# One store per layer moved from SyncE's queue to GpSimd's

## The chip, the cores and the metric

The kernel runs on 1 core of one Trainium2 chip. Its engines are TensorE (PE in the profile; PEld is its loading of weights), VectorE (DVE), ScalarE (ACT), GpSimd (POOL) and SyncE (SP). Each has its own list of instructions; SP only starts transfers. SP, ACT and POOL each start DMAs from their own queue, and 16 DMA engines carry them out. The metric is device microseconds of an execution.

## The reference

The input x has 8 batches of 512 tokens with 256 values. There are two layers, and each is a mixer followed by a mixture of experts; each adds its result to x:

```python
x = x + _L0_attn_a_ref(_layernorm(x, axis=-1), ...)   # a scan with decay 0.9 over the tokens
x = x + _L0_ffn_ref(_layernorm(x, axis=-1), ...)      # 16 experts, 4 chosen, and a shared one
x = x + _L0_attn_b_ref(_layernorm(x, axis=-1), ...)   # causal attention, 16 heads
x = x + _L0_ffn_ref(_layernorm(x, axis=-1), ...)
```

The mixture of experts is what matters here. The router chooses 4 of 16 experts for every token; a shared pair of experts works on all of them:

```python
h = jnp.einsum('td,edf->etf', x, gate_w)
u = jnp.einsum('td,edf->etf', x, up_w)
y = jnp.einsum('etf,efd->etd', jax.nn.silu(h) * u, down_w)
routed = jnp.einsum('etd,te->td', y, combine)
sh = jax.nn.silu(x @ sh_gate_w) * (x @ sh_up_w) @ sh_down_w
return (routed + sh).reshape(hidden_states.shape)
```

## The kernel before, in words

The kernel works in four stages: a *stretch* and a *routed* stage for each layer.

A stretch (`stretch`) goes through the 8 batches. For each it does the mixer (scan in the first layer, attention in the second), norms the result, computes the router's choices, and scatters each token's row into a table in device memory, `xg`, sorted by expert (POOL, indirect DMAs at L662). The sum after the mixer is stored to the first of two tables in device memory, `parts[i][0]` (SP, L1209). The shared experts (`shared_experts`) run two batches later: products with the gate and up weights (L908), their activation (L921 to L927), the product with the down weights into the accumulator tile `pd_m` (L936), two ACT copies of it into the tile `ys_m` (L944), and the store of `ys_m`, 512 KB, into the second table, `parts[i][1]` (L945). So 8 such stores belong to each layer. The last one stands at the end of the stretch: after it the list of blocks is ready (`blocks`), and nothing else of the stretch is left.

A routed stage (`routed`) reads a count of blocks on every engine (L886), skips a branch for a rare surplus of blocks (L889), and goes through 136 blocks of 128 sorted rows. For each block SP reads where its rows lie (L779, a register load for four blocks at a time) and loads them into a tile `rows` (L793); ACT and DVE copy the expert's weights into `gate` and `up` (L801); PE transposes the rows (L808), ACT copies the result (L809), PE multiplies with gate and up (L819), ACT and DVE form the activation (L827 to L829), PE multiplies with the down weights (L847), ACT scales (L855), and POOL adds the rows into `parts[i][0]` or `parts[i][1]`, by turns, with an indirect accumulating DMA (L856). At the start the first two blocks' rows are loaded at once, and both blocks are transposed on PE ahead of the first product.

The order on each engine is made when the program is built, from the order in the source and a planner's estimates; waits between engines are semaphores that are put in by what each instruction reads and writes. Tiles come from pools with a fixed number of buffers: `ys_m`, the shared experts' activations `act_m` and the `rows` tiles share one pool of 9 buffers (`kb4`), so that a new tile waits until the last use of its buffer's former holder is over. Each DMA signals its completion on one of 8 semaphores by turns, with one set of 8 for SP's and ACT's queues and another for POOL's.

Of the kernel before, what the change touches and what calls it, by code (L numbers as in the profile page):

```python
# [16 lines left out]
B, T, D = 8, 512, 256  # L17
# [57 lines left out]
def tile_hybrid_block(  # L75
# [22 lines left out]
    nc = tc.nc  # L98
# [8 lines left out]
    def bank(shape, name: str, kind: str = "one"):  # L107
        kind = instead.get(kind, kind)
        return stage[kind].tile(shape, FP, tag=kind, name=name)
# [15 lines left out]
    parts = [[dram.tile([NTOK + BLK, D], FP, name=f"part_{i}_{j}") for j in range(2)] for i in range(2)]  # L125
# [11 lines left out]
    def rows_of(part, b: int):  # L137
        return part[b * T : (b + 1) * T, :].rearrange("(t p) d -> p t d", p=P)
# [51 lines left out]
    def load_expert(e: int):  # L190
# [13 lines left out]
        out=before,  # L204
        in_=before,
# [17 lines left out]
    def load_attention_weights():  # L223
# [16 lines left out]
        out=causal, in_=causal, compare_op=ALU.is_ge, fill=0.0, base=0, pattern=[[0, 2], [1, P]], channel_multiplier=-1  # L240
# [6 lines left out]
        out=tri, in_=tri, compare_op=ALU.is_gt, fill=0.0, base=0, pattern=[[1, P]], channel_multiplier=-1  # L247
# [162 lines left out]
    def kb4(name: str):  # L410
        return work.tile([P, NT, D], FP, tag="kb4", name=name, bufs=KB)
# [481 lines left out]
    def shared_experts(i: int, b: int, xnT_of, tanh: bool):  # L893

        tag = f"m{i}_{b}"

        def steps():
            xnT = xnT_of()
            acts = []
            for n in range(NSH):  # L900
                _, g_sb, u_sb, _ = shared[n]
                act = work.tile([P, KF, T], FP, tag="kb4", name=f"act_{tag}_{n}", bufs=KB)
                acts.append(act)
                for f in range(KF):
                    pair = [bank([P, T], f"pg_{tag}_{n}_{f}_{which}") for which in range(2)]
                    for dst, w in zip(pair, (g_sb, u_sb)):
                        for k in range(KD):
                            nc.tensor.matmul(  # L908
                                dst,
                                lhsT=w[:, k, f * P : (f + 1) * P],  # L910
                                rhs=xnT[:, k, :],
                                start=(k == 0),
                                stop=(k == KD - 1),
                            )
                        if dst is pair[0]:
                            yield KD * T
                    ph, pu = pair
                    sig = work.tile([P, T], FP, tag="col", name=f"sig_{tag}_{n}_{f}", bufs=COLS)
                    if tanh:

                        nc.scalar.activation(sig, ph, AF.Tanh, scale=0.5)  # L921
                        nc.vector.scalar_tensor_tensor(sig, sig, 1.0, ph, ALU.add, ALU.mult)
                        nc.vector.scalar_tensor_tensor(act[:, f, :], sig, 0.5, pu, ALU.mult, ALU.mult)
                    else:
                        nc.scalar.activation(sig, ph, AF.Sigmoid)
                        nc.vector.tensor_mul(sig, ph, sig)
                        nc.vector.tensor_mul(act[:, f, :], pu, sig)  # L927
                    yield KD * T
            y_sb = kb4(f"ys_{tag}")
            for half in range(2):  # L930
                py = bank([P, 2, D], f"pd_{tag}_{half}")
                for j in range(2):
                    t = 2 * half + j
                    for n in range(NSH):
                        for f in range(KF):
                            nc.tensor.matmul(  # L936
                                py[:, j, :],
                                lhsT=acts[n][:, f, t * P : (t + 1) * P],
                                rhs=shared[n][3][:, f, :],
                                start=(n == 0 and f == 0),  # L940
                                stop=(n == NSH - 1 and f == KF - 1),
                            )
                    yield NSH * KF * D
                nc.scalar.copy(y_sb[:, 2 * half : 2 * half + 2, :], py)  # L944
            nc.sync.dma_start(out=rows_of(parts[i][1], b), in_=y_sb)  # L945

        return Piece(NSH * KF * (2 * KD * T + NT * D), steps())


# [485 lines left out]
```

## Time and profile before

| | us |
|---|---|
| median of 3 runs (lowest, highest) | 1792.99 (1790.45, 1796.93) |
| the profiled execution, its own time | 1789.56 |
| its span, first to last instruction | 1787.8 |
| PE busy | 1686.6 |
| DVE busy | 1094.7 |
| ACT busy | 806.1 |
| POOL busy | 769.6 |
| the last store of the first layer's shared sums starts | 375.06 |
| the last store of the second layer's | 1356.90 |

The mean granted clock of PE over the span is 0.975 of full speed. Times in the profile are microseconds from the span's start. A row of the timeline has the start, the length, the engine, the source line, the operation, what it writes and reads, how often, and in brackets how long the engine was idle before it and what ended that. Lines marked SPq, ACTq or POOLq are of an engine's sequencer (starting a DMA, waiting, loading a register), which are not counted as busy. A DMA's landing is the time from the start of its issue to the last of its completion signals. The profile names at each wait the signal that came last.

### The profile page before, as it was taken

The page shows a single profiled execution, that of the slowest core. Times are in us where ns is not written, and L with a number is a line of the kernel's source. Part 1 is how long each engine was busy: PE and PEld are TensorE (multiplying, and loading weights), DVE is VectorE, ACT ScalarE, POOL GpSimd, SP SyncE. Part 2 cuts the span into 40 slices and gives each one's busy share as a digit, 9 for nine tenths or more (in the row PEclk, how much of TensorE's full clock was granted, in tenths as well). Part 3 has the DMA queues.
Part 4 walks back from the last instruction along what each step waited for, and adds up shares of the span by engine and source line. Part 5 has one row for each costly group of instructions (what it writes and reads, how often), then busy time and mean ns, then how long its engine had stood idle before and what let it go on. Part 6 is the DMA issues. An engine that isn't in the chain of part 4 may idle for free. (4 is left out here: it accounts for less than half of the span.)

```text
span 1787.8 us, 32810 instructions
## 1 busy us (share of the span) xinstructions
PE 1686.6 (94%) x10640; PEld 1261.9 (71%) x10640; DVE 1094.7 (61%) x3399; ACT 806.1 (45%) x1740; POOL 769.6 (43%) x675
## 2 busy tenths in 40 slices
PE   5899999989999999979999999999998999999993
PEld 3566566569999999954445455455467999998993
DVE  5877777535555655546776675756653665565552
ACT  2322222135555555545654554544413555555552
POOL 4255554625555655540022422312442555555563
PEclk9899999999999999989999999999999999999997
DMA  5443322535555655540012112112443555566666
GB/s 167 154 148 133 130 78 84 198 76 94 97 95 102 111 98 95 96 89 10 28 50 73 63 61 73 51 60 80 149 172 78 93 98 94 110 125 122 127 122 177
DMA packets 149999, 181.37 MB, mean 101 GB/s; under 512 B 16097, under 2 KB 136961, under 8 KB 149825
## 3 DMA queue, kind: packets, MB, share of 16 engines
q0 software_dynamic: 54432, 81.53, 24.2%
q1 hardware_dynamic: 93600, 93.50, 17.6%
q10 hardware_dynamic: 1792, 4.19, 0.6%
q8 instruction: 89, 1.46, 0.3%
q14 instruction: 86, 0.70, 0.1%
HBM read 81.62 MB, written 97.53 MB: 100 GB/s over the span
## 5 line engine op out<-in xcount | busy, mean ns | idle before, releaser
L856 POOL DMA_INDIRECT part<-rows x272 | 427.0, 1570 | 370.0 <-ACT rows L855 291.4
L662 POOL DMA_INDIRECT xg<-sorted_m,slots_m x256 | 255.7, 999 | 283.4 <-ACT slots_m L659 116.6
L819 PEld LDWEIGHTS ph<-rows,gate 128*128 128x128 f32 x2176 | 286.3, 193 | 16.5 <-ACT rows L809 2.1
L819 PE MATMUL ph<-rows,gate 128*128 128x128 f32 x2176 | 290.0, 277 | 0.6 <-ACT rows L809 0.6
L819 PE MATMUL ph<-rows,up 128*128 128x128 f32 x2176 | 288.7, 276 | 0.0
L847 PE MATMUL pyr<-w_all,rows 128*128 x1088 | 280.5, 380 | 0.4 <-DVE rstd_l L398 0.4
L819 PEld LDWEIGHTS ph<-rows,up 128*128 128x128 f32 x2176 | 266.3, 193 | 0.0
L827 ACT ACTIVATE rows<-ph 128x256 f32<-128x256 f32 x272 | 104.2, 383 | 329.6 <-PE ph L819 329.6
L828 DVE TENSOR_TENSOR rows<-ph,rows 128x256 f32<-128x256 f32 x272 | 115.2, 423 | 190.3 <-ACT rows L827 190.0
L847 PEld LDWEIGHTS pyr<-w_all,rows 128*128 128x128 f32 x1088 | 185.2, 191 | 14.6 <-ACT rows L855 0.7
L801 ACT COPY gate<-w_all 128x512 f32 x272 | 170.0, 626 | 14.6 <-SPq L889 2.6
L1053 ACT ACTIVATE w_all<-ps_a 128x1024 f32<-128x1024 f32 x128 | 124.4, 1021 | 80.3 <-PE ps_a L1042 72.7
L801 DVE COPY up<-w_all 128x512 f32 x272 | 120.1, 442 | 33.0 <-PE ph L819 18.0
L855 ACT ACTIVATE rows<-pyr,gain 128x256 f32<-128x256 f32 x272 | 128.4, 472 | 14.7 <-PE pyr L847 13.2
L908 PE MATMUL pg_m<-xT_m,su_sb 128*128 128x512 f32 x256 | 131.4, 637 | 0.0
L832 DVE SCALAR_TENSOR_TENSOR gain<-rows,expert_b 128x4 f32<-128x4 f32 x272 | 61.2, 225 | 112.3 <-ACT rows L855 83.4
L1042 PE MATMUL ps_a<-w_all 32*128 32x512 f32 (+3 forms) x1024 | 122.1, 472 | 7.0 <-ACT w_all L1053 5.6
L908 PE MATMUL pg_m<-xT_m,sg_sb 128*128 128x512 f32 x256 | 123.0, 603 | 0.0
L936 PE MATMUL pd_m<-sd_sb,act_m 128*128 128x256 f32 x512 | 120.9, 385 | 0.0
L808 PE MATMUL pt<-ident,rows 128*128 128x128 f32 x544 | 105.1, 275 | 16.4 <-DMA rows<-xg 16.4
L829 DVE TENSOR_TENSOR rows<-ph,rows 128x256 f32<-128x256 f32 x272 | 115.1, 423 | 8.3
L936 PEld LDWEIGHTS pd_m<-sd_sb,act_m 128*128 128x128 f32 x512 | 97.1, 192 | 21.6 <-issue 4.7
(219 smaller groups left out, 2216.2 us busy)
## 6 DMA issues: line engine op xcount, KB each, us to landing
rows<-xg SPq DMA_DIRECT2D x272, 136.0 KB, 2.6
part<-x SPq DMA_DIRECT2D x16, 512.0 KB, 2.8
part<-ys_m SPq DMA_DIRECT2D x16, 512.0 KB, 2.8
w_all<-in_L_ffn_gate_w_dram SPq DMA_DIRECT2D x24, 256.0 KB, 5.2
w_all<-in_L_ffn_up_w_dram SPq DMA_DIRECT2D x24, 256.0 KB, 5.5
w_all<-in_L_ffn_down_w_dram SPq DMA_DIRECT2D x24, 256.0 KB, 5.9
sum<-part POOLq DMA_DIRECT2D x10, 512.0 KB, 4.2
xg<-zeros SPq DMA_DIRECT2D x34, 136.0 KB, 2.2
```

The lines of the kernel that those rows point to most:

```text
L662: nc.gpsimd.indirect_dma_start(out=xg[i], out_offset=bass.IndirectOffsetOnAxis(ap=slots[:, at : at + 1], axis=0), in_=rows[:, t, :], in_of ...
L801: copy(here, w_all[:, bass.ds(held[n][0] + half * KD * F, KD * F)])
L819: nc.tensor.matmul(ph[:, s, f * P : (f + 1) * P], lhsT=both[s][:, k * F + f * P : k * F + (f + 1) * P], rhs=rows[:, ROW + k * P : ROW + (k ...
L828: nc.vector.tensor_mul(act, ph[:, 0, :], act)
L829: nc.vector.tensor_mul(act, ph[:, 1, :], act)
L847: nc.tensor.matmul(py, lhsT=act[:, f * P : (f + 1) * P], rhs=w_all[:, bass.ds(w + 2 * KD * F + f * D, D)], start=(f == 0), stop=(f == KF - 1),
L855: nc.scalar.mul(rows[:, 0:D], py, gain[:, TK : TK + 1])
L856: nc.gpsimd.indirect_dma_start(out=parts[i][n % 2], out_offset=bass.IndirectOffsetOnAxis(ap=rows[:, D + 2 * TK : D + 2 * TK + 1].bitcast(U ...
L908: nc.tensor.matmul(dst, lhsT=w[:, k, f * P : (f + 1) * P], rhs=xnT[:, k, :], start=(k == 0), stop=(k == KD - 1),)
L936: nc.tensor.matmul(py[:, j, :], lhsT=acts[n][:, f, t * P : (t + 1) * P], rhs=shared[n][3][:, f, :], start=(n == 0 and f == 0), stop=(n == ...
L1042: nc.tensor.matmul(ps[j // 2][:, j % 2, col : col + n], lhsT=k_sb[w][r, o, c * P : (c + 1) * P], rhs=q_sb[r, o, c * P : T], start=True, st ...
L1053: nc.scalar.activation(es[two], ps[two][:, :, 0:cols], AF.Exp, scale=ATT_SCALE)
```

## The change

In each layer the last batch's `ys_m` is stored by POOL's queue; the other seven remain on SP's. What is stored and where stays the same.

```diff
                 nc.scalar.copy(y_sb[:, 2 * half : 2 * half + 2, :], py)
-            nc.sync.dma_start(out=rows_of(parts[i][1], b), in_=y_sb)
+
+            (nc.gpsimd if b == B - 1 else nc.sync).dma_start(out=rows_of(parts[i][1], b), in_=y_sb)
 
         return Piece(NSH * KF * (2 * KD * T + NT * D), steps())
```

In the built program the store is taken out of SP's list, where it stood ahead of the load of the block count (L886), and put into POOL's, between the last scatter (L662) and the load of the block count there. ACT's list is the same. In PE's list one register load (L772) moves past one block's down products in each layer, and in DVE's list a few small neighbours near the start of each routed stage change places. The completion semaphores that later DMAs use move on by one on POOL's queue and back by one on SP's.

## The prediction

> **What bounds the kernel now.** I read the page first: its span, the busy shares, the chain that ended last. Then, because the change touches one store per layer, the timeline of SyncE (SP) and TensorE (PE) around the end of each stretch, and last the durations and landings of DMAs of 512 KB by queue.
>
> ```profile
> span 1787.8 us, 32810 instructions
> PE 1686.6 (94%) x10640; PEld 1261.9 (71%) x10640; DVE 1094.7 (61%) x3399; ACT 806.1 (45%) x1740; POOL 769.6 (43%) x675
> PE 21%; DMA 2%; ACT 0%; issue 0%; SPq 0%; DVE 0%; ACTq 0%; POOL 0%; POOLq 0%; DVEq 0%
> ```
>
> PE is busy 94% of the span, so an edit on queues is worth what it does to PE's idle stretches. Of those over 5 us there are three in the trace; two are the ones right behind the moved store. The chain is named for the last 430 us alone; followed back it ends at the second of these two. This is its start, in order of time (start, length, what):
>
> ```profile
> 1358.47 1.13 SPq L779
> ...
> 1360.02 0.35 SPq L793
> ...
> 1360.94 2.05 DMA rows<-xg
> 1362.99 0.14 issue
> 1363.13 0.66 PE pt L808 x2
> ```
>
> The reader is to see that the chain runs over SP: a register load (L779), the loads of the first two blocks of sorted rows (L793), the second one's landing, and then PE's second pair of transposes (L808). The second block's landing decides, not the first's: in PE's order both blocks are transposed ahead of the first product (L819). The same stretch, timeline of SP, then of PE, then of PE after the first layer:
>
> ```profile
> 1356.90 0.38 SPq L945 DMA_DIRECT2D part<-ys_m  x1
> 1360.02 4.10 SPq L793 DMA_DIRECT2D rows<-xg  x5
> ```
> ```profile
> 1362.31 0.66 PE L808 MATMUL pt<-ident,rows 128*128 128x128 f32 x2 [6.06 <-DMA rows<-xg]
> 1363.13 0.66 PE L808 MATMUL pt<-ident,rows 128*128 128x128 f32 x2 [0.16 <-DMA rows<-xg]
> ```
> ```profile
> 380.39 0.66 PE L808 MATMUL pt<-ident,rows 128*128 128x128 f32 x2 [5.98 <-DMA rows<-xg]
> 381.31 0.66 PE L808 MATMUL pt<-ident,rows 128*128 128x128 f32 x2 [0.26 <-DMA rows<-xg]
> ```
>
> In layer 1 the store goes out at 375.06, the two loads at 378.15 and 379.08, the second lands at 381.17. From there on PE is the bound (100.00 us busy of the 100 from 400 to 500, 120.00 of the 120 from 1380 to 1500), so a shift of this start reaches the end one for one, once in each layer.
>
> **The change part by part.**
>
> *Removed from SP: one wait and one issue per layer.* SP's store waits for ScalarE's last copy (L944, ends 1356.87) and takes 0.38 us. Behind it stand the load of the block count (L886, 0.28), a branch with its semaphore waits (L889, 0.7 us in all) and the 1.13 us load of the row numbers: 3.12 us from the store's start to the first rows. Their data has been ready since about 1344. Without the store SP runs through all this while PE still multiplies, and stands at the first rows load, which by the built program waits for PE's last product (its buffer held an operand). PE ends at about 1356.25, so the first rows load goes at about 1356.4 in place of 1360.02: 3.6 us earlier.
>
> *The second rows load gains none of it by right.* It takes the buffer of the stored sum itself: in the built program it waits for the store's completion. Before, that store was long enough ago: it landed 3.41 us after 1356.90, at 1360.31, and SP came at 1360.94. After, SP will stand there waiting, so the start is: store's start + its landing + about 0.2 (in the routed stage a row load followed the landing that freed its buffer, 396.46, at 396.66) + 2.1 (landing of the load, 2.05 to 2.16). This replaces a wait of SP on SP by one on GpSimd's (POOL's) queue. Queued behind it on SP are the third and later rows loads, due on PE only after two blocks of products, at 1368.6: slack of over 3 us.
>
> *Added to POOL: one wait and one issue per layer.* The store stands behind the last scatter (L662, over at 364.7 and 1346.5) and ahead of the block count and branch; the first accumulate (L856) comes at 392.41 and 1373.19, so 16 us cover the store's issue on POOL, and would have to be used up before it costs. Behind the store stands also POOL's step that credits its skipped semaphores (1.0 and 1.6 us), for which the third rows load waits; about 1 us of load and branch and this step end near 1360, before that load is due.
>
> *The unknown: how long a 512 KB store takes from POOL's queue to land.* No row shows this store there. Rows, by source line (landing as min/median/max):
>
> ```profile
> L1327 POOL DMA_DIRECT2D out_dram<-sum x5: 1167/1173/1328, 1577.2 to 1761.4; - x5
> DMA to landing us min/median/max: 4.0/4.6/4.6
> ```
> ```profile
> L1317 POOL DMA_DIRECT2D sum<-part x10: 585/588/1182, 1555.6 to 1748.0; - x10
> DMA to landing us min/median/max: 3.8/4.2/5.3
> ```
> ```profile
> part<-ys_m SPq DMA_DIRECT2D x16, 512.0 KB, 2.8
> x<-part POOLq DMA_DIRECT2D x2, 512.0 KB, 4.4
> ```
>
> Lower end 2.75 (the quickest landing of the same store from SP; a queue that issues in 0.36 us is no slower than one that takes 0.6 to 1.3, unless the trace hides it). Upper end 5.3 (the longest 512 KB on POOL's queue). I take 4.4: the two kinds nearest are the writes L1327 (4.0 to 4.6, other row length) and the loads L1150 (4.3 to 4.6, same 128x4x256 shape, other direction).
>
> Layer 1: 375.1 + 4.4 + 0.2 = 379.7 against 379.08: +0.6 us. Layer 2: 1356.95 + 4.4 + 0.2 = 1361.55 against 1360.94: +0.6. Sum +1.2 us. At 2.75 it is -1.0 each, -2.1; at 5.3 it is +1.5 each, +3.0. The break-even is a landing of 3.8 us.
>
> A page states a rule against this change: in the Trainium skill, "SBUF — State Buffer", section "SBUF: two separate sides", a VectorE fp32 copy between SBUF places locks GpSimd out of writing descriptors until the copy ends. Two such copies (L801, 375.22 for 0.76 us) lie on top of the new store; by the rule its issue would start at about 376.1, about 1 us later, and the sum would be some +3.2. The trace's nearest case does not show it: the load L1150 at 759.01 began inside a pair of these copies (758.28 for 0.95) and took 0.82 us and 4.3 us to land, like its three fellows. "DMA: Bandwidth & Descriptors", section "Specifications", puts the first byte at some 1 us from GpSimd and 0.6 from SyncE; by that difference alone the landing would be 3.2, and the sum -1.2. The landings above (2.6 from SP, 4.0 to 4.6 from POOL for L1327) show more.
>
> *PE's clock.* After each gap PE runs at half clock for a while. Windows of PE (columns: stretch, length, busy of PE, its weight loads, VectorE, ScalarE, POOL, then granted clock, DMA share, GB/s):
>
> ```profile
> 381.00:388.00 7.00, 6.74 (x39) 6.72 (x38) 2.66 (x11) 1.76 (x5) 0.00 (x0) 0.60 0.53 138
> 1362.00:1370.00 8.00, 7.23 (x44) 6.55 (x45) 3.35 (x13) 2.98 (x8) 0.00 (x0) 0.73 0.49 139
> ```
>
> That is 7 x 0.40 + 8 x 0.27 = 2.8 + 2.2 = 5.0 us lost. The change puts the first two transposes (0.33 to 0.66 us) into the middle of the gap, at about 1358.7, and leaves some 4 us idle behind them. I take no change; the bounds are one step of 3.41 us (the shortest stretch at half clock in the trace) more or less per layer, 1.7 us of work each.
>
> *Moved elsewhere.* The order on ScalarE is the same; PE and VectorE swap a few neighbours early in each routed stage (a register load and one block's products, two tiny reductions). Their cost is nothing while PE is continuously fed there; without that cover it would be tens of ns.
>
> *The sum.* The profiled execution took 1789.56 us, 1.76 beyond its span; with +1.2 it would be 1790.8. It lies 3.4 us under the median of the runs shown, 1792.99 (1790.45 to 1796.93), so against the median: 1794.2.
>
> **The rivals.**
>
> *Slower.* The store on POOL's queue lands so late that the start of both routed stages slips. Place: SP's second rows load of each layer. It decides from 3.8 us on; to cost 0.3% (5.4 us) it needs 3.8 + 2.7 = 6.5 us. For it: loads on POOL's queue at the start took 5.9 to 6.1, and one 512 KB store from SP 6.59 among other traffic. Against it: no 512 KB transfer on POOL's queue took over 5.3, and DMA is a third to a half busy here. At 6.59: +2.8 each, +5.6, 1798.6.
>
> *Faster.* The store lands as from SP and the gap gets so short that PE keeps its clock: -2.1 - 5.0 = -7.1, 1785.9. It decides where the landing is under 3.8 and the gap left behind the first transposes under some 2 us. For it: SP's 3.6 us are really freed, and behind a gap of 1.80 us (ends 49.77) the clock stayed whole for the next 2.4 us. Against it: a gap of 2.96 us (ends 214.02) still brought half clock, and no landing of 512 KB on POOL's queue is under 3.8.
>
> *It does nothing.* The second rows load waits for the same completion as before in effect: landing 3.6 to 4.0, within 0.4 us of 1793.0. This lies inside the forecast.
>
> **How the numbers follow.** What a measurement of this kernel can tell from no change is about 0.3%, 5.4 us. Forecast, with doing nothing in it, 0.76: its working runs from -2.1 to +3.0 and stays inside 0.3% even with one clock step. Slower rival 0.15, faster rival 0.09; each takes in what is beyond 0.3% for reasons I have not seen. Range: the working's ends with one clock step (-3.8 to +4.7) on the median, and the spread of a median of a few runs, about 1 us more: 1788 to 1799. It reaches both rivals' near sides and leaves out their far ones.
>
> **What would show it.** In the profile after: the store among POOL's instructions, L944's end to its start under 0.2 us, landing 4.0 to 4.6; on SP the first rows load at PE's last product, some 3.6 us earlier against it, and the second one 3 to 5 us behind the first; PE's gap in two parts, about 2.5 and 4 us; the first product of each routed stage 0.6 us later against the end of the stretch than now (7.3 us from PE's last product to the first L819). Wrong if the second rows load does not wait for the store, if the landing is outside 2.75 to 5.3, if the half-clock stretch changes by more than a step, or if a stage away from the store changes length.

## The result, and the profile after

| | median us | runs | ratio to before, 95% interval |
|---|---|---|---|
| before | 1791.49 (1786.24 to 1796.93) | 12 | |
| changed | 1791.88 (1789.08 to 1798.05) | 12 | 1.0000 (0.9988 to 1.0013) |

The interval is about 2 us wide on either side, so the change made no difference that this measurement can tell. The forecast, 1794.2 us, is 2.3 us above the median; 1.5 us of that is its base, the median of 3 executions (1792.99) where that of 12 is 1791.49. The profiled execution of the changed kernel took 1789.08 us, against 1789.56.

The head of the page and the chain that ended last, of the changed kernel:

```profile
span 1787.4 us, 32810 instructions
PE 1685.7 (94%) x10640; PEld 1260.1 (71%) x10640; DVE 1094.5 (61%) x3399; ACT 805.9 (45%) x1740; POOL 772.8 (43%) x677
PE 47%; DMA 2%; issue 2%; DVE 1%; POOL 1%; ACT 1%; ACTq 0%; POOLq 0%; DVEq 0%; SPq 0%
```

PE is as busy as before to 1 us. The chain is now followed back far past the start of the second routed stage, so the shares can't be set beside those of before. Its part at that stage says what became of the wait (start, length, what):

```profile
1361.61 0.02 POOLq L886
1361.63 3.24 DMA part<-ys_m
...
1365.01 2.12 DMA rows<-xg
1367.12 0.14 issue
1367.26 0.66 PE pt L808 x2
```

Before, the chain came to the second rows load over SP's register load; now it comes over the landing of the moved store. SP's own work is off the path, and the store is on it.

The timelines of POOL, ACT and PE of the changed kernel, at the end of the first layer's stretch and then of the second's (start, length, engine, line, what, and in brackets the idle time before):

```profile
376.07 0.59 ACT L944 COPY ys_m<-pd_m 128x512 f32<-128x512 f32 x1 [1.53 <-PE pd_m L936]
376.95 0.98 POOL L946 DMA_DIRECT2D part<-ys_m  x1 [10.48 <-ACTq L889]
379.07 0.41 PE L808 MATMUL pt<-ident,rows 128*128 128x128 f32 x2 [3.04 <-DMA rows<-xg]
383.55 0.66 PE L808 MATMUL pt<-ident,rows 128*128 128x128 f32 x2 [4.06 <-DMA rows<-xg]
```
```profile
1360.75 0.59 ACT L944 COPY ys_m<-pd_m 128x512 f32<-128x512 f32 x1 [1.53 <-PE pd_m L936]
1361.63 0.83 POOL L946 DMA_DIRECT2D part<-ys_m  x1 [10.49 <-ACTq L889]
1362.99 0.41 PE L808 MATMUL pt<-ident,rows 128*128 128x128 f32 x2 [2.28 <-DMA rows<-xg]
1367.26 0.66 PE L808 MATMUL pt<-ident,rows 128*128 128x128 f32 x2 [3.85 <-DMA rows<-xg]
```

PE's one gap of 6 us has become two, of 3.04 and 4.06 us in layer 1 and of 2.28 and 3.85 us in layer 2, with the first block's transposes between them. Counted from the end of PE's last product of the stretch, in us:

| | layer 1 before | layer 1 after | layer 2 before | layer 2 after |
|---|---|---|---|---|
| store starts | 0.65 | 0.92 | 0.65 | 0.92 |
| its landing, from its start | not in the trace | 3.89 | 3.41 | 3.24 |
| first rows load starts | 3.74 | 0.03 | 3.77 | 0.03 |
| second rows load starts | 4.67 | 5.29 | 4.69 | 4.30 |
| first product (L819) starts | 7.35 | 7.96 | 7.33 | 7.00 |
| second block's last product ends | 13.43 | 13.38 | 12.36 | 12.10 |

So the first product comes 0.61 us later in layer 1 and 0.33 us earlier in layer 2: together +0.28 us. The second block is done 0.05 and 0.26 us earlier.

Away from the store the two profiles differ by more than this. PE's last product of the first stretch ends at 374.41 us before and at 376.03 after, and the last stage, from PE's last product of the second stretch to the end of the span, takes 431.6 and 426.7 us. The changed kernel profiled again, on another chip, has 376.17 and 432.8 us. So these are differences between executions, and a whole time cannot show +0.28 us.

PE's granted clock, in windows of the changed kernel at about the same distance from PE's last product as those of before (stretch, length, busy of PE, its weight loads, VectorE, ScalarE, POOL, then clock, DMA share, GB/s):

```profile
382.62:389.62 7.00, 6.08 (x38) 6.10 (x38) 2.60 (x11) 1.43 (x4) 0.00 (x0) 0.65 0.52 154
1366.46:1374.46 8.00, 6.90 (x45) 6.64 (x46) 3.12 (x12) 2.77 (x7) 0.00 (x0) 0.74 0.43 126
```

The clock is 0.65 and 0.74 against 0.60 and 0.73. The stretch at half clock is 6.83 us long at each of the two starts, before and after; the moved store changed none by a step.

### The profile page after: what moved, and what is told of

Read it like the earlier page. It is cut to its first block, busy times and chain, and to the rows that moved or that the text cites. A ratio compares the mean times of both kernels' runs of the same rounds, so it can differ in the third digit from the quotient of the medians.

```text
span 1787.4 us, 32810 instructions
## 1 busy us (share of the span) xinstructions
PE 1685.7 (94%) x10640; PEld 1260.1 (71%) x10640; DVE 1094.5 (61%) x3399; ACT 805.9 (45%) x1740; POOL 772.8 (43%) x677
## 4 chain that ended last, share of the span: by engine, by line
PE 47%; DMA 2%; issue 2%; DVE 1%; POOL 1%; ACT 1%; ACTq 0%; POOLq 0%; DVEq 0%; SPq 0%
PE ph L819 14%; PE pyr L847 6%; PE ps_a L1043 5%; PE pg_m L908 5%; PE po_a L1078 4%; PE pd_m L936 2%; PE pq_a L988 2%; PE pt L808 2%; PE pv_a L1006 2%; PE py_a L421 2%; PE pl_m L546 1%; POOL xg L662 1%; PE pto_a L1094 1%; DMA part<-rows 1%; DMA sum<-part 0%
## 5 line engine op out<-in xcount | busy, mean ns | idle before, releaser
L662 POOL DMA_INDIRECT xg<-sorted_m,slots_m x256 | 256.3, 1001 | 284.6 <-ACT slots_m L659 118.3
L819 PEld LDWEIGHTS ph<-rows,gate 128*128 128x128 f32 x2176 | 285.6, 192 | 16.5 <-ACT rows L809 2.1
L819 PE MATMUL ph<-rows,gate 128*128 128x128 f32 x2176 | 289.3, 276 | 0.6 <-ACT rows L809 0.6
L819 PE MATMUL ph<-rows,up 128*128 128x128 f32 x2176 | 288.8, 276 | 0.0
L819 PEld LDWEIGHTS ph<-rows,up 128*128 128x128 f32 x2176 | 266.3, 193 | 0.0
L801 ACT COPY gate<-w_all 128x512 f32 x272 | 170.1, 627 | 14.9 <-PE ph L819 2.4
L801 DVE COPY up<-w_all 128x512 f32 x272 | 120.5, 444 | 33.9 <-PE ph L819 18.8
L855 ACT ACTIVATE rows<-pyr,gain 128x256 f32<-128x256 f32 x272 | 128.7, 473 | 15.8 <-PE pyr L847 14.3
```

Of the source, the lines that this page charges most:

```text
L662: nc.gpsimd.indirect_dma_start(out=xg[i], out_offset=bass.IndirectOffsetOnAxis(ap=slots[:, at : at + 1], axis=0), in_=rows[:, t, :], in_of ...
L801: copy(here, w_all[:, bass.ds(held[n][0] + half * KD * F, KD * F)])
L819: nc.tensor.matmul(ph[:, s, f * P : (f + 1) * P], lhsT=both[s][:, k * F + f * P : k * F + (f + 1) * P], rhs=rows[:, ROW + k * P : ROW + (k ...
L855: nc.scalar.mul(rows[:, 0:D], py, gain[:, TK : TK + 1])
```

## The experiments

Every ratio below is to the kernel before on the same chip. The chips differ (the kernel before has medians of 1813.67, 1796.83 and 1818.69 us on the three used here), so times of different groups are not to be set side by side. Distances in us are from the end of PE's last product of the stretch, as in the table above.

The theory to be tested: SP is really freed, but the second rows load waits for the landing of the moved store, since its tile takes the buffer of `ys_m`; that takes back what was gained. The main rival: the freed SP is worth nothing in any case, because something else holds the start.

**The stored tile in a buffer of its own.** The changed kernel, and then the kernel before (store on SP), with `ys_m` of the last batch in the pool of the scan's values, so that no rows tile waits for the store:

```diff
-            y_sb = kb4(f"ys_{tag}")
+            if b == B - 1:
+                y_sb = values(f"ys_{tag}")[:, 0 : NT * D].rearrange("p (t d) -> p t d", t=NT)
+            else:
+                y_sb = kb4(f"ys_{tag}")
```

> The changed kernel, with the last sum of each layer in a buffer of another pool (that of the attention's v tiles, idle then), so that no early rows load waits for the store to land. Theory (the second rows load waited for the store on POOL's queue, and this ate SyncE's freed time): both rows loads go at PE's last product, the second about 0.9 us behind the first, PE's first gate product comes some 3.5 us behind the last product of the stretch instead of 7.0 and 8.0, so 3.5 to 4.5 us less per layer, 7 to 9 us in all, and up to 5 more if PE keeps its clock: ratio 0.992 to 0.996 to the kernel before. Rival (the start is bound by something else, for instance the register loads on PE or ScalarE): nothing, 1.000.

Measured: 0.9964 (0.9945 to 0.9982), 1806.69 us against 1813.67. PE in the second layer of this kernel:

```profile
1376.18 0.41 PE L808 MATMUL pt<-ident,rows 128*128 128x128 f32 x2 [1.30 <-DMA rows<-xg]
1377.17 0.41 PE L808 MATMUL pt<-ident,rows 128*128 128x128 f32 x2 [0.58 <-DMA rows<-xg]
1378.73 2.08 PE L819 MATMUL ph<-rows,gate 128*128 128x128 f32 x8 [1.15 <-ACT rows L809]
```

The gap of 3.85 us is gone: the second pair of transposes comes 0.58 us behind the first. The two rows loads start at -0.83 and 0.03 us, the first product at 3.85 us (layer 1: 3.97) in place of 7.00 (7.96). That is 7.1 us over both layers; the ratio is 6.5 us of 1813.67 (3.3 to 10.0). In layer 1 the clock record has no half-clock stretch at this start (PE's gaps were 1.62 and 1.58 us), and the second block's last product ends at 7.80 us in place of 13.38; in layer 2 a stretch of 3.41 us is left, and it ends at 9.12 in place of 12.10.

> The kernel before, with the same other buffer for the last sum and the store left on SyncE. Theory (before, the store stood ahead of the rows loads in SyncE's order and had landed by the time SyncE came to the second one): the buffer changes nothing, the second rows load still goes about 4 us behind the store's start, the first product 7.3 us behind the last product of the stretch; ratio 1.000. Rival (the shared buffer was what held the start before as well): 7 us less, 0.996.

Measured: 0.9998 (0.9980 to 1.0016), first product at 7.43 and 7.36 us. With the store on SP the buffer is worth nothing. Moving the store alone is worth nothing either (1.0000). Both together are worth 0.36%: each removes one of two waits that end at nearly the same time.

**The other side of the same wait.** The first two blocks' rows tiles in that pool in place of the store's tile, with the store on POOL's queue and then on SP's:

```diff
-            rows = work.tile([P, 4 * D], FP, tag="kb4", name=f"rows_{i}_{n}", bufs=KB)
+            if n < 2:
+                rows = xv(f"rows_{i}_{n}")[:, 0 : 4 * D]
+            else:
+                rows = work.tile([P, 4 * D], FP, tag="kb4", name=f"rows_{i}_{n}", bufs=KB)
```

(`xv` is another name for `values`.)

> The changed kernel, with the rows of the first two blocks of each layer in the v pool's buffers; the order on all engines stays the same. Now neither of the two loads waits for PE or the store. Theory (SyncE is free once the store is on POOL's queue): both go once the last scatter has landed, some 10 us before PE's last product, PE's gap is bounded by ScalarE's branch and its first gate copy, the first product comes about 2.5 us behind the last one, 4.5 to 5.4 us less per layer, 9 to 11 us in all, and up to 5 more by the clock: ratio 0.991 to 0.995. Rival (something else of the changed order binds, so the freed time is worth little): under 3 us, above 0.998.

Measured: 0.9968 (0.9946 to 0.9989). The two loads now go out 6.3 to 12.5 us ahead of PE's last product, and yet the first product comes at 3.95 and 3.81 us, not at 2.5. The sign is the theory's, the size is not: the expectation counted one gate copy of ScalarE ahead of the first product, and overlooked that two more stand there. ACT and then PE in layer 1 of this kernel (L814 and L824 here are L809 and L819 elsewhere, L806 is L801):

```profile
390.21 1.66 ACT L806 COPY gate<-w_all 128x512 f32 x3 [1.35 <-PE pt L813]
391.77 0.64 ACT L814 COPY rows<-pt 128x256 f32<-128x256 f32 x2
```
```profile
389.55 0.63 PE L813 MATMUL pt<-ident,rows 128*128 128x128 f32 x4 [1.31 <-DVE up L806]
392.19 1.07 PE L824 MATMUL ph<-rows,gate 128*128 128x128 f32 x4 [2.01 <-ACT rows L814]
```

The transposes are over at 390.2, but ACT copies three blocks' gate weights before it copies the transposed rows, and PE waits 2.01 us for that. This is the bound that comes next here.

> The kernel before, with the rows of the first two blocks in the v pool's buffers and the store left on SyncE. Theory (SyncE's in-order wait for the store's data is the bound of the kernel before): the two loads still go 3.1 and 4.0 us behind the store's start, the first product 7.3 us behind the last; ratio 1.000. Rival (the buffers alone bring the gain, the queue is beside the point): as the changed kernel with these buffers, 0.991 to 0.995.

Measured: 1.0011 (0.9996 to 1.0026), first product at 7.36 and 7.38 us. As with the store's buffer, nothing without the move.

**The store twice on POOL's queue.** The landing of the second one takes the place of the first one's for the second rows load:

```diff
             (nc.gpsimd if b == B - 1 else nc.sync).dma_start(out=rows_of(parts[i][1], b), in_=y_sb)
+            if b == B - 1:
+                nc.gpsimd.dma_start(out=rows_of(parts[i][1], b), in_=y_sb)
```

> The changed kernel, with the last sum of each layer stored twice in a row from POOL's queue; the second store waits for the first to land, and the second rows load for both. Theory (the landing of the store passes one for one to the end): the second rows load comes one more landing later, 3.2 to 4.0 us per layer, 6.5 to 8 us in all, and up to one clock step (1.7 us) per layer more: ratio 1.003 to 1.006. Rival (the start has slack in the routed stage): under 2 us, 1.000 to 1.001.

Measured: 1.0061 (1.0036 to 1.0085). POOL and then PE in the second layer of this kernel:

```profile
1370.75 0.82 POOL L946 DMA_DIRECT2D part<-ys_m  x1 [10.63 <-ACTq L889]
1374.28 0.78 POOL L948 DMA_DIRECT2D part<-ys_m  x1 [2.70 <-DMA part<-ys_m]
```
```profile
1372.14 0.66 PE L808 MATMUL pt<-ident,rows 128*128 128x128 f32 x2 [2.31 <-DMA rows<-xg]
1380.27 0.66 PE L808 MATMUL pt<-ident,rows 128*128 128x128 f32 x2 [7.47 <-DMA rows<-xg]
```

The second store waits for the first, and PE's second gap grows from 3.85 to 7.47 us (layer 1: 4.06 to 7.35). The first product comes at 11.76 and 10.89 us, 3.8 and 3.9 us later than with one store. Against the kernel before the first product is 4.4 + 3.6 us later, and the second block is done 3.5 and 4.7 us later (at 16.98 and 17.02 us), together 8.2. The stretches at half clock grow too, from 6.83 us each to 10.24 and 13.65, but PE idles through most of what is added, so up to the second block this costs next to nothing more. The ratio is +10.9 us of 1796.83 (6.5 to 15.3), which holds these 8 us. What is above them stays open: the profile is of the slowest of the five executions (1817.76 us, median 1808.49). A later landing does pass to the end; the rival's under 2 us is ruled out.

**The store on ScalarE's queue.** One word of the moved line, `nc.scalar` in place of `nc.gpsimd`:

> The store of the last sum from ScalarE's queue instead of POOL's. Theory (what the change gains on SyncE is lost by POOL's later start and longer landing): the store starts under 0.1 us behind ScalarE's copy and lands in 2.8 to 3.4 us, so the second rows load goes 3.1 to 3.6 us behind the copy (from POOL 4.7 and 3.7, from SyncE 4.05 by its own chain): 0.5 to 1.0 us per layer less than the kernel before, ratio 0.999, not to be told from 1. ScalarE's first gate copies come about 0.4 us later, which costs nothing. Rival (the issue on ScalarE delays the first copies of weights): 0.5 us more per layer, 1.0005.

Measured: 1.0007 (0.9993 to 1.0020). The store starts at 0.65 us in both layers, takes ACT's queue 0.38 us, and lands 4.08 and 3.13 us later; the first product comes at 7.93 and 6.63 us. The expectation missed in layer 1, where the landing is outside 2.8 to 3.4 us and the first product comes 0.58 us later than in the kernel before; in layer 2 it comes 0.70 us earlier. So the difference between the layers is not POOL's: 3.89 and 3.24 us from POOL, 4.08 and 3.13 from ACT. ACT in layer 1 of this kernel shows what the store costs there:

```profile
376.10 0.38 ACTq L946 DMA_DIRECT2D part<-ys_m  x1
378.76 1.14 ACT L801 COPY gate<-w_all 128x512 f32 x2 [2.69 <-DMA part<-ys_m]
```

The first gate copy begins 3.31 us behind PE's last product in place of 2.00: 1.3 us later, where 0.4 was expected, mostly because ACT's load of the block count (L886) now stands behind the store. The two copies end at 4.45 us, ahead of the second block's transposes at 7.47, so this costs nothing here. (The bracket names the store's landing, but that comes only at 4.73 us.)

**Up copies away from VectorE.** The first two blocks' up weights are copied by ScalarE, so that no VectorE copy lies on the store's issue:

```diff
-            for half, (copy, name) in enumerate(((nc.scalar.copy, "gate"), (nc.vector.tensor_copy, "up"))):
+            up_copy = nc.scalar.copy if n < 2 else nc.vector.tensor_copy
+            for half, (copy, name) in enumerate(((nc.scalar.copy, "gate"), (up_copy, "up"))):
```

> The changed kernel, with the first two weight copies of each layer that VectorE makes (up) put on ScalarE, so that VectorE is idle during POOL's store. Rule (VectorE's copies lock GpSimd out of writing descriptors): the store's issue on POOL falls below 0.83 us in both layers and its landing below 3.2 us. Rival (the copies do not matter to the landing): issue 0.8 us and more and landing within 3.2 to 3.9 us as in the changed kernel.

Measured in one execution (1796.21 us, where the kernel before has a median of 1796.83); POOL in its layer 1:

```profile
378.71 0.83 POOL L947 DMA_DIRECT2D part<-ys_m  x1 [10.63 <-ACTq L890]
```

The issue in layer 1 takes 0.83 us in place of 0.98 (layer 2: 0.82, against 0.83), the store still starts 0.30 us behind ScalarE's copy, and the landing is 4.37 and 3.23 us; layer 1's lies outside what either side expected. VectorE's copies lengthen POOL's issue by 0.15 us in layer 1; they are neither the later start nor the longer landing.

**The changed kernel again.**

> The changed kernel once more, for the spread of the store's start and landing on POOL's queue between executions. Theory: the store starts about 0.3 us behind ScalarE's copy and lands 3.2 to 3.9 us later, and the first product stands 7.0 to 8.0 us behind the last product of the stretch in both layers. Rival (the difference of the two layers is a fixed one): 3.9 in the first layer and 3.2 in the second again, to 0.1 us.

Measured in one execution (1794.27 us): landings of 4.03 and 3.23 us, first products at 8.13 and 7.07. Layer 1 lies a little outside both expectations (to 3.9 and 8.0 us, and 3.9 to 0.1). The layers stand apart as in the first profile (3.89 and 3.24), so this is no chance of one execution.

**Past the next bound.** With both buffers apart (the stored tile, and the second block's rows), and then with the first two blocks' transposed rows copied by VectorE:

```diff
-            nc.scalar.copy(rows[:, ROW : ROW + D], pt.rearrange("p k q -> p (k q)"))
+            (nc.vector.tensor_copy if n < 2 else nc.scalar.copy)(rows[:, ROW : ROW + D], pt.rearrange("p k q -> p (k q)"))
```

> The changed kernel, with the last batch's shared sum of each layer in a buffer of the pool that the scan's values use, and the second block's rows of each routed stage in that pool as well; the first block's rows stay in the 9-buffer pool. So neither of the two first loads waits for the store. Theory (ScalarE's order is the new bound once the store's landing is out of the way): the transposes are done by about 2 us after PE's last product, and the first product still comes at 3.8 to 4.0 us, behind three gate copies and the copy of the first transposed rows on ScalarE; ratio to the kernel before 0.9955 to 0.998, as with the store's buffer alone. Rival (the second rows load had been the bound there too): the first product moves to 2.5 to 3 us, ratio 0.9935 to 0.995.

Measured: 0.9953 (0.9930 to 0.9975), first product at 4.01 and 3.83 us. In layer 2 the transposes are done at 2.73 us and ScalarE's order alone holds the product, as the theory says. In layer 1 the second block's rows, loaded at -0.26 us, land only at 3.63; PE's second transposes, which stand ahead of the first product, wait for them until 3.77, and ScalarE's copy of the first rows ends at 3.90. So there two waits end at nearly the same time.

> As the kernel with both buffers apart, but the copies of the first two blocks' transposed rows (L809) go to VectorE in place of ScalarE. Theory (ScalarE's order is the bound): the first product waits for the first gate copy alone, which ends 2.45 to 2.6 us after PE's last product, so it comes at 2.6 to 2.9 us in both layers, 1.1 us earlier than with ScalarE; ratio to the kernel before 0.994 to 0.997, about 0.0012 below the other. Rival (VectorE's own order holds the copies: two up copies and the small gain steps stand ahead): the first product stays at 3.5 us or later, and the ratio is that of the other kernel.

Measured: 0.9941 (0.9915 to 0.9967), medians of 1806.46 and 1818.69 us (the ratio is not their quotient); the first product comes at 4.06 and 3.29 us, not at 2.6 to 2.9. In layer 2 it moved by 0.54 us, half of what was expected. VectorE and then PE in layer 1 of this kernel show why it did not move there:

```profile
387.52 0.22 DVE L837 SCALAR_TENSOR_TENSOR gain<-rows,expert_b 128x4 f32<-128x4 f32 x1
389.31 0.22 DVE L837 SCALAR_TENSOR_TENSOR gain<-rows,expert_b 128x4 f32<-128x4 f32 x1 [1.58 <-DMA rows<-xg]
389.46 0.15 DVE L845 TENSOR_REDUCE gain<-gain 128x1 f32<-128x4 f32 x1
389.52 0.41 DVE L814 COPY rows<-pt 128x256 f32<-128x256 f32 x1
```
```profile
389.32 0.41 PE L813 MATMUL pt<-ident,rows 128*128 128x128 f32 x2 [1.40 <-DMA rows<-xg]
```

The first block was transposed by 387.92, but its copy stands on VectorE behind a small step on the second block's rows, which land at 389.2. So the rival's mechanism held in layer 1. PE's own second transposes wait for the same landing and stand ahead of the first product, so another order on VectorE could have brought it at most 0.35 us there, PE's last wait ahead of the product. The two kernels' intervals overlap, so the better of them is not settled; the one with VectorE's copies is the fastest of these by its ratio. Its whole interval lies below that of the changed kernel too (0.9988 to 1.0013, on another chip).

## Why the prediction was right, step by step

The forecast (within 0.3%, +1.2 us) held, and its mechanism was the one at work: one wait was exchanged for another of nearly the same length. The time, known to 2 us either way, could not have told +1.2 us from nothing; it is the order of the waits that bears the mechanism out. By the first products the sum was +0.28 us, and layer 2 moved the other way than forecast. Its steps:

- *SP is freed and the first rows load goes at PE's last product.* Right: 0.03 us behind it, where 3.6 us earlier was forecast and 3.7 was measured (3.74 and 3.77 to 0.03).
- *The second rows load waits for the store's completion.* Right: SP stands 4.30 us (layer 1) and 3.65 us (layer 2) in the wait ahead of it. With the stored tile or the rows tiles in another buffer it is gone, and 0.32 to 0.36% with it.
- *Start of that load = store's start + landing + about 0.2.* The form was right, two terms were mis-sized. The landing was put at 4.4 us, and was 3.89 and 3.24. Both rows that it came from lie in busier stages (DMA share 0.65 from 570 to 580 and 0.81 from 1610 to 1618 us, against 0.51 from 376 to 381 and 0.34 from 1356 to 1362 at the two starts). The trace held a nearer case: SP's stores of the same tile, 2.8 us where nothing disturbs them, with 0.45 us for POOL's longer issue (0.82 by L1150), are 3.25. The prediction used their quickest as its lower end only. The start was put at under 0.2 us behind ScalarE's copy, and was 0.30, where SP and ACT needed 0.03. What follows the landing took 0.48 in layer 1 (380.85 to 381.33) and 0.14 in layer 2. The sum by these terms is +0.62 and -0.39 us for the load (5.29 against 4.67, 4.30 against 4.69), where +0.6 each was forecast; layer 1 is right because the errors cancel (+0.2 for the start and +0.3 for what follows the landing, -0.5 for the landing), which is luck.
- *VectorE's copies against POOL's issue.* By the Trainium skill, "SBUF — State Buffer", section "SBUF: two separate sides", GpSimd can't write its descriptors while such a copy runs, which the prediction put at 1 us. Here 0.15 us of it showed: an issue of 0.98 us with the copies on it, 0.83 without.
- *The landing that the pages would have given.* By the Trainium skill, "DMA: Bandwidth & Descriptors", section "Anatomy of one DMA — SWDGE (gpsimd) path", a transfer from GpSimd's queue takes about 2.0 us and the bytes at 436 GB/s, by a fit; for 524288 bytes that is an estimate of 3.2 us. Layer 2 has 3.23 and 3.24, so it was nearer than the rows that were chosen, as was the 3.2 that the prediction worked out from the first byte and set aside; layer 1 has 3.89 and 4.03.
- *The clock unchanged.* Right: 6.83 us at half clock at each start, before and after. The split of the gap, forecast as 2.5 and 4, was 3.04 and 4.06 in layer 1, where the first rows load took 2.9 us to land and not 2.1, and 2.28 and 3.85 in layer 2.
- *The rivals.* The slower one needed a landing of 6.5 us; the longest of this store from POOL's queue in any run was 4.37. Its mechanism is real, as the doubled store shows. The faster one had half its condition met in layer 2 (landing under 3.8), but the gap behind the first transposes stayed at 3.85 us, not under 2, and the half-clock stretch stayed. Its mechanism is real too: with the stored tile in its own buffer the gaps were 1.62 and 1.58 us in layer 1, and there was no such stretch.

## What sets the landing

The trace's records of packets split each store's time into three parts. In us from the start of the issue, with the transfers of instructions (the DMA queues of kind "instruction") that run while the store's data moves:

| store | issue | first packet | data moves for | landing | instruction fetches during the data |
|---|---|---|---|---|---|
| SP, before, layer 2, two batches earlier (1308.61) | 0.37 | 0.90 | 1.51 | 2.81 | none |
| SP, before, layer 2 | 0.38 | 0.92 | 2.08 | 3.41 | one of 0.35 |
| ACT, layer 2 | 0.38 | 1.02 | 1.69 | 3.13 | one of 0.31, at the end |
| POOL, layer 2 | 0.83 | 1.39 | 1.42 | 3.24 | none |
| POOL, layer 2, again | 0.82 | 1.40 | 1.41 | 3.23 | none |
| POOL, layer 1 | 0.98 | 1.55 | 1.97 | 3.89 | one of 0.60 |
| POOL, layer 1, again | 0.98 | 1.55 | 2.11 | 4.03 | one of 0.71 |

The first packet comes about 0.55 us behind the end of the issue from SP and POOL alike; POOL's is 0.47 us later because its issue is 0.45 us longer. How long the data moves goes with the fetches. Six of the eight stores in the second layer's stretch of the kernel before have none, move their data in 1.50 to 1.51 us and land after 2.79 to 2.89; the two with one, the last among them, take 1.88 and 2.08, and 3.26 and 3.41. The 16 of both layers:

```profile
DMA to landing us min/median/max: 2.8/2.8/3.4
```

So without a fetch POOL's store lands about 0.4 us later than SP's, nearly all of it the issue; its data moves only 0.09 us faster (1.41 to 1.42). That the two landings are close here, 3.24 and 3.41 us, goes with the fetch in SP's. The packets differ, in windows from the issue to the landing, of the kernel before and then of the changed kernel in layer 2 (queue: packets, MB, share of 16 engines; issues with KB each and time to landing):

```profile
q1 hardware_dynamic: 528, 0.52, 43.4%
part<-ys_m SPq DMA_DIRECT2D x1, 512.0 KB, 3.4
```
```profile
q0 software_dynamic: 144, 0.52, 39.5%
part<-ys_m POOLq DMA_DIRECT2D x1, 512.0 KB, 3.2
```

The same 0.52 MB is 512 packets of 1 KB and 16 small ones from SP, and 128 packets of 4 KB and 16 small ones from POOL.

The small packets, as many as there are DMA engines, come last. From POOL in layer 2 all 16 end between 2.64 and 2.82 us behind the start of the issue. From SP before, 15 end between 2.28 and 2.43 and one at 3.01; from POOL in layer 1, 14 between 2.81 and 2.97 and two at 3.33 and 3.52.

In layer 1 the data takes 0.55 and 0.70 us longer, and in both runs a transfer of 8 KB of instructions, of 0.60 and 0.71 us, falls into that time. Late packets that are one to three of 16 fit a fetch that holds up single DMA engines, and with them the last of the store's data. The records used here do not say which engine a packet went through, and no kernel took the fetch away, so this stays an inference. The length of a fetch does not give the length of the delay: in SP's store before, one of 0.35 us goes with 0.57 us more than without; in the run with the rows in the v pool, layer 2, one of 0.36 with 0.89; in the run without VectorE's copies, one of 0.36 and the ends of two others (0.55 and 1.56) with 1.1.

## What to carry to other kernels

Taking a transfer off a busy queue pays only if nothing behind it needs that transfer's completion: here the next load on the freed queue reused the stored tile's buffer, and the wait on the queue became a wait for the landing, at nearly the same time. Look up which buffer the next tile takes before moving a store, and free both at once: either alone gave 0 here, both gave 0.36%. What came next was the order on ScalarE, in layer 1 together with the landing of the second rows load. For the length of a transfer on another queue, take the same transfer as it is, undisturbed, and add the difference of the issues (2.8 + 0.45 us here, against 3.24 measured), before taking another transfer of that queue from a busier stage; and allow for what runs beside it (0.65 to 1.13 us more in layer 1).

## What the runs showed of the hardware that was not expected

- POOL starts this waiting store 0.30 us behind the copy that releases it, in every run; SP and ACT start it 0.03 us behind. The trace before has the like: ScalarE's L855 ends at 392.13, and the accumulate that waits for it starts at 392.41.
- A 512 KB store in rows of 1 KB goes out in packets of 4 KB from POOL's queue and of 1 KB from SP's. With no fetch of instructions in it, its data moved in 1.41 to 1.42 us from POOL and 1.50 to 1.51 from SP; POOL's longer issue (0.83 against 0.37 us) makes its landing the later one, 3.23 to 3.24 against 2.79 to 2.89.
- Each store in the table with a fetch within its data landed later than the same queue's without one: 3.41 against 2.81 from SP, 3.89 and 4.03 against 3.24 from POOL.
- One of the two pays where VectorE's up copies and POOL's issue overlap. In layer 1 VectorE's first copy begins 0.10 us ahead of the issue, which then takes 0.98 us in place of 0.83, and the copies keep their 0.43 us. In layer 2 it begins 0.02 us ahead, the issue takes 0.83, and the second copy 0.72 us.
- In layer 1 of the kernel with VectorE's transposed copies PE's gaps were 1.49, 1.40 and 0.35 us, and the clock record has no half-clock stretch there: the second block's last product ended at 7.87 us, against 9.43 with ScalarE's copies (gaps of 1.49 and 1.86 us, one stretch of 3.41 us) from nearly the same first product (4.06 and 4.01 us). With the stored tile alone in its own buffer it was as in the first of these: gaps of 1.62 and 1.58 us, no stretch, 7.80 us.
